# Layer 0's keys and values one chunk later, and whole steps for the empty attention steps at a layer's end

## The chip, the cores and the metric

The kernel runs on one core of one Trainium2 chip. The metric is the device time of one execution in microseconds (us); three runs were timed, and one more execution was profiled. Engines are named TensorE (PE in the profile, its weight loads PEld), VectorE (DVE), ScalarE (ACT), GpSimd (POOL) and SyncE (SP).

## The reference

Two layers of a transformer on a graph: 2708 nodes with 512 features, eight heads of 64, and a 0/1 adjacency matrix with some nine neighbours a node. Each layer is, with its own weights:

```python
q = (h @ Wq.T + bq).reshape(n, 8, 64)      # k and v likewise
scores = einsum('nhd,mhd->hnm', q, k) / sqrt(64)
scores = where(mask == 0, -1e9, scores)    # mask = adj + I
ctx = einsum('hnm,mhd->nhd', softmax(scores), v).reshape(n, 512)
h1 = layer_norm(h + ctx @ Wo.T + bo)
h2 = layer_norm(h1 + relu(h1 @ W1.T + b1) @ W2.T + b2)
```

The second layer takes h2 of the first. Everything is float32.

## The kernel before

**Tiles, blocks and chunks.** The nodes are sorted by their number of neighbours and cut into 22 tiles of 128 (the last has 20). Two tiles make a block (list `blocks`); a layer works through eleven blocks, numbered k = 0 to 10, and each block goes through the feed-forward network in 16 chunks, numbered f = 0 to 15: a chunk is 128 of the 2048 hidden units. One chunk on TensorE is four matmul calls into a PSUM tile `pf` (L1596 in the plain blocks, L1780 in the others); ScalarE evicts it with the ReLU (L1607 or L1791). The output is then summed in PSUM from the evicted chunks. In blocks 0, 1 and 10 of layer 0 that is plain (`feed_forward`, L1569). In blocks 2 to 9 it is done with seven products in place of eight for each pair of chunks (`feed_forward_by_seven`): VectorE makes sums of the evicted chunks (L1746 to L1749), and TensorE multiplies them with prepared combinations of W2, the forms (L1769), which SyncE loads from DRAM (L1731). The first products come behind chunk 5, the second behind chunk 7, and so on. In these blocks the PSUM tiles of the chunks and those of all projections and flips have two buffers each (`places_of_psum(3 - seven, ...)`), in the plain blocks three.

**What runs beside the chunks.** The loop over k and f (the body of `by_edges`) is a schedule written by hand: the engines take their instructions in the order in which the program writes them. After each chunk it writes some of these:

- The attention of later tiles, a generator (`attend`), driven by `advance(credit)`: each chunk has a credit (tables PACE, PACES, PACE7), and each step taken costs what `attend` yields, the number of gathered rows over two. A step gathers the keys and values of up to two neighbours per node (GpSimd, L1119), multiplies and sums the keys with the query on VectorE (L1156, then the scores sc, L1162), and, for the step before, takes exponentials (L1175) and weighs a part of the values on ScalarE (L1182), the rest on VectorE (L1188, L1195). When a tile is complete, VectorE sums it up (L1203 to L1218), and one step later ScalarE divides it (cx, L1226). Since each step ends the work of earlier ones, three empty steps stand behind the second tile of the order and behind the last one; an empty step costs 0.2. After the last, two small instructions set a flag (L1951).
- The output projection of the next block (`attended`, chunks 10 to 13): the attention result cx is flipped by TensorE transposes (tp, L1349), copied out of PSUM to cT by ScalarE (L1354) and multiplied with Wo (o, L626, or L621 for the 20-row tile). `until(g)` runs the attention until tile g is divided.
- In layer 0, the keys and values of the block behind (`keys_values`), a generator of four steps, taken behind chunks 5, 6, 7 and 8: flip both tiles of the normalized rows h (tp, L1349) and copy them to zT (L1354, eight pieces); project keys (k) and values (v) of the first tile (L626), evict them on VectorE (L1881) and ScalarE (L1886), and store zT and h (SyncE, L1888, L1889); the same for the second tile; scatter the rows of both tiles to DRAM (GpSimd, L1082). h comes out of VectorE's normalization (L1290) of the block that just ended.

Of the kernel before, what the change touches and what calls it, by code (L numbers as in the profile page):

```python
# [37 lines left out]
SLOTS = 2  # L38
# [449 lines left out]
def by_edges(ctx: ExitStack, tc: tile.TileContext, x, xT, adj, layers, out, redo):  # L488
# [639 lines left out]
    def asked(n, g):  # L1128

        r = size(g)  # L1130
        if g in own:
            return own.pop(g)
        if n == 0 and not all_made:
            return None
        q = at.tile([P, DM], F32, tag="q", name="q", bufs=QB)
        fetch(n, q, q_d[n], g)
        return q

    def chunks_of(g):
        S = CAPS[g]  # L1140
        k = (S + SLOTS - 1) // SLOTS
        cuts = [-(-S * i // k) for i in range(k + 1)]
        return [(g, a, b - a) for a, b in zip(cuts, cuts[1:])]
# [102 lines left out]
    def loads(n):  # L1246

        ready = []
        for g, s0, c in (chunk for g in order for chunk in chunks_of(g)):
            r = size(g)  # L1250
            kv = rows_of_keys(n)
            for s in range(s0, s0 + c):
                load = gather(kv[:r, s - s0, :], kv_d[n], idx[:r, g, s : s + 1])
                for move in written[n]:
                    tc.add_manual_dep(
                        load.ins,
                        move.ins.name,
                        mybir.DependencyInfo(
                            mybir.DependencyClass.Sync, mybir.DependencyReason.DATA
                        ),  # L1260
                        reason="every row of keys is in its place",
                    )
                written[n].clear()
            ready.append(kv)
            if len(ready) > EARLY:
                yield ready.pop(0)
        yield from ready
# [638 lines left out]
    order = [g for block in blocks for g in block]  # L1906

    def attend(n, got):

        peak = small.tile([P, NT], F32, tag="peak", name="peak", bufs=1)  # L1910
        nc.vector.memset(peak, 0.0)
        loaded = loads(n)
        steps = []
        for g in order:
            cuts = chunks_of(g)
            steps += [(g, s0, c, i, i + 1 == len(cuts)) for i, (_, s0, c) in enumerate(cuts)]
            if g == order[1]:
                steps += [None] * 3
        steps += [None] * 3
        kv = next(loaded)  # L1920
        yield 0.0
        q, later = asked(n, order[0]), None
        done = [None] * 3
        for k, step in enumerate(steps):
            if step:
                g, s0, c, i, last = step
                if i == 0:
                    while q is None:
                        q = asked(n, g)
                        if q is None:  # L1930
                            yield None
                    t, q = Tile(g, q), None
                if k > 0:
                    kv = next(loaded)
                t.weights(kv, s0, c)
                if q is None and g != order[-1]:
                    q, later = later or asked(n, order[order.index(g) + 1]), None
                if g == order[-3] and i == 2:
                    later = asked(n, order[-1])
                done.append((t, kv, s0, c, last))  # L1940
            else:
                done.append(None)
            t3, t2, t1 = done[-4:-1]
            if t1:
                t1[0].weigh(*t1[1:4])
            if t2 and t2[-1]:
                t2[0].sums(peak)
            if t3 and t3[-1]:
                got[t3[0].g] = t3[0].divided()
            yield c / SLOTS if step else 0.2  # L1950
        nc.vector.tensor_reduce(flags[:, 4 + n : 5 + n], peak, AX.X, ALU.max)  # L1951
        nc.vector.tensor_scalar(
            flags[:, 4 + n : 5 + n], flags[:, 4 + n : 5 + n], SAFE, None, ALU.is_le
        )
# [30 lines left out]

    got = {}
    ahead = attend(0, got)
    early = {}

# [38 lines left out]
    behind, pool = None, []  # L2028
    for n in range(NL):
        last = n == NL - 1  # L2030
        nxt = None if last else Layer(n + 1, layers[n + 1])
        if n > 0:
            streamed = now.queries(order[10:16])
            got = {}
            ahead = attend(n, got)
            for j in (5, 6):
                now.query(*pool.pop(0))
# [40 lines left out]
        for k, block in enumerate(blocks):  # L2078
            more = k + 1 < NB
# [13 lines left out]
            for f, zs in enumerate(working):  # L2093
# [4 lines left out]
                        added_row(h, size(g), now.e1b2)  # L2098
                if tail and f in TAILS[k > FORMED[n] + 1]:
                    next(tail)  # L2100
                if f in (5, 6, 7, 8) and behind:
                    next(behind)
                if more and n == 0 and f == 5 + 2 * (k == 0):
                    xbs = now.residuals(blocks[k + 1])
# [75 lines left out]
            if not last:  # L2180
                behind = now.keys_values(block, zs)
            if more:
                hs = hs_next
        if not last:
# [9 lines left out]
            behind = None  # L2194
# [7 lines left out]
def gnn_transformer(tc: tile.TileContext, x, xT, adj, layers, out):  # L2202

    nc = tc.nc
    with tc.tile_pool(name="result", bufs=1) as result:
        redo = result.tile([1, 1], I32, name="redo")  # L2210
        again = by_edges(tc, x, xT, adj, layers, out, redo)
        with tc.If(again > 0):
            by_rows(tc, x, xT, adj, layers, out)
# [41 lines left out]
```

## Time and profile before

| | |
|---|---|
| time, median of 3 runs | 1817.57 us (1815.81 to 1818.39) |
| profiled execution, its own time | 1817.08 us |
| its span from first to last instruction | 1815.1 us |
| mean granted clock of TensorE | 0.998 |
| ScalarE, VectorE, GpSimd busy | 55%, 81%, 47% of the span |
| moved by DMA | 426.74 MB, mean 235 GB/s |

A row of the timeline gives the start in us from the span's start, the duration, the engine, the line, the operation with output<-input, and the count of instructions merged; in brackets the idle time of the engine just before, and what ended it. A matmul's duration overlaps the next one's, so what a matmul takes of TensorE is read from start to start. A row of the list of waits gives the waiting operation, what it waited for, then the total in us, the times and the longest.

### The profile page before, as it was taken

Reading aid. Unit: us, or ns where it says so; the run is one execution under the profiler, and the core shown is the slowest. Engines: PE = TensorE matmul, PEld = TensorE weight load, DVE = VectorE, ACT = ScalarE, POOL = GpSimd, SP = SyncE. Lnnn points to the kernel's source line nnn. Section 1 sums busy time; section 2 is a strip of 40 time slices with the busy share of each in tenths; the row PEclk is TensorE's granted clock in tenths of the full one; section 3 lists DMA queues with packets and bytes.
Section 4 is the critical chain, followed back from the end, with each engine's and each line's share of the span. In section 5 each row is a group of like instructions: output and inputs, shape, how many; then the busy total and the mean of one; then the engine's idle time right before and its main releaser. Section 6 shows DMA issues by size and latency. Waiting matters only on the chain. (4 is left out here: it accounts for less than half of the span.)

```text
span 1815.1 us, 23887 instructions
## 1 busy us (share of the span) xinstructions
PE 1791.5 (99%) x6839; PEld 1214.6 (67%) x6839; DVE 1463.3 (81%) x2599; ACT 1001.1 (55%) x3397; POOL 855.4 (47%) x830
## 2 busy tenths in 40 slices
PE   9999999999999999999999999999999999999997
PEld 4444456666777867777677644666666888788786
DVE  4987778988989889799896267988888899989933
ACT  5771436645555555555653104677776677767631
POOL 3333755534454544454540132556665665655312
PEclk9999999999999999999999999999999999999999
DMA  9997987757676675666752777967867787877531
GB/s 335 369 344 252 374 284 245 230 181 241 203 238 220 203 259 192 208 220 202 241 194 73 242 285 272 319 193 256 279 186 263 243 264 237 293 225 234 173 94 36
DMA packets 186728, 426.74 MB, mean 235 GB/s; under 512 B 20550, under 2 KB 83898, under 8 KB 186584
## 3 DMA queue, kind: packets, MB, share of 16 engines
q0 software_dynamic: 76992, 264.49, 44.0%
q1 hardware_dynamic: 99434, 139.01, 22.5%
q10 hardware_dynamic: 10158, 21.61, 3.1%
q8 instruction: 56, 0.92, 0.2%
q14 instruction: 88, 0.72, 0.1%
HBM read 357.13 MB, written 57.11 MB: 228 GB/s over the span
## 5 line engine op out<-in xcount | busy, mean ns | idle before, releaser
L1119 POOL DMA_INDIRECT kv<-kv_d,listed x420 | 526.0, 1252 | 307.2 <-DVE acc L1195 145.8
L1780 PE MATMUL pf<-hT,w 128*128 128x256 f32 x1792 | 407.2, 379 | 2.1 <-ACT ft L1791 2.1
L1780 PEld LDWEIGHTS pf<-hT,w 128*128 128x128 f32 x1792 | 339.2, 190 | 59.2 <-issue 11.0
L1182 ACT ACTIVATE kv<-kv,p 128x64 f32<-128x64 f32 x1232 | 311.0, 335 | 5.0
L1156 DVE TENSOR_TENSOR kv<-kv,q 128x1024 f32<-128x1024 f32 (+1 forms) x222 | 257.1, 1158 | 14.1 <-DMA q<-q_d,ident_i 10.9
L1162 DVE TENSOR_REDUCE sc<-kv 128x16 f32<-128x1024 f32 (+1 forms) x222 | 258.0, 1162 | 7.6
L1195 DVE TENSOR_TENSOR acc<-acc,kv 128x1024 f32<-128x1024 f32 (+2 forms) x178 | 205.6, 1155 | 49.6 <-ACT kv L1182 36.9
L1596 PEld LDWEIGHTS pf<-hT,w 128*128 128x128 f32 x1024 | 178.5, 190 | 55.3 <-issue 34.6
L1596 PE MATMUL pf<-hT,w 128*128 128x256 f32 (+1 forms) x1024 | 214.6, 357 | 0.1
L1791 ACT ACTIVATE ft<-pf,b 128x256 f32<-128x256 f32 x168 | 78.1, 466 | 214.1 <-PE pf L1780 211.4
L1569 PE MATMUL a<-w,ft 128*128 128x512 f32 x416 | 194.6, 592 | 0.0
L1175 ACT ACTIVATE p<-sc,listed 128x8 f32<-128x8 f32 x420 | 103.6, 295 | 127.9 <-DVE sc L1162 116.5
L1281 POOL TENSOR_TENSOR rd<-va,mhalf 128x1 f32<-128x1 f32 (+1 forms) x48 | 43.8, 913 | 230.8 <-DVE va L1279 230.7
L626 PE MATMUL o<-wo,cT 128*128 128x512 f32 x336 | 151.0, 593 | 0.3 <-ACT cT L1354 0.3
L1188 DVE TENSOR_TENSOR kv<-kv,p 128x512 f32<-128x512 f32 (+1 forms) x178 | 123.6, 694 | 4.8 <-ACT p L1175 4.5
L1569 PEld LDWEIGHTS a<-w,ft 128*128 128x128 f32 x416 | 77.7, 190 | 57.5 <-issue 52.0
L626 PEld LDWEIGHTS o<-wo,cT 128*128 128x128 f32 x336 | 63.4, 190 | 69.3 <-issue 59.6
L1331 POOL TENSOR_SCALAR va<-sq 128x1 f32<-128x1 f32 (+1 forms) x40 | 17.2, 429 | 188.4 <-ACT xb L1324 101.9
L751 DVE MAX8 tops<-code 128x8 f32<-128x247 f32 (+2 forms) x242 | 78.8, 400 | 28.0 <-ACT code L746 27.9
L1226 ACT ACTIVATE cx<-acc,su 128x64 f32<-128x64 f32 (+1 forms) x352 | 88.2, 333 | 11.2 <-DVE su L1218 6.2
L1182 ACT ACTIVATE acc<-kv,p 128x64 f32<-128x64 f32 (+1 forms) x352 | 88.8, 335 | 1.4
L746 ACT ACTIVATE code<-aj 128x1354 bf16<-128x1354 int32 (+1 forms) x44 | 73.5, 1724 | 23.7 <-POOL aj L740 19.0
(258 smaller groups left out, 2793.8 us busy)
## 6 DMA issues: line engine op xcount, KB each, us to landing
forms<-form_d SPq DMA_DIRECT2D x294, 128.0 KB, 3.8
aj<-in_adj SPq DMA_DIRECT2D x42, 677.0 KB, 6.3
kv_d<-kvs ACTq DMA_DIRECT2D x21, 512.0 KB, 7.4
h<-ln_b POOLq DMA_DIRECT2D x41, 256.0 KB, 7.0
xg<-in_xT SPq DMA_DIRECT2D x19, 512.0 KB, 8.0
w<-in_W SPq DMA_DIRECT2D x16, 512.0 KB, 6.4
kv<-kv_d,listed POOLq DMA_INDIRECT x420, 6.5
zT_d<-zT SPq DMA_DIRECT2D x22, 256.0 KB, 5.3
```

The source lines that it names most:

```text
L626: nc.tensor.matmul(o[:r], xs(c), wm[:, c, :], start=(c == 0), stop=(c == NC - 1))
L1119: return nc.gpsimd.indirect_dma_start(out=to, out_offset=None, in_=table[:, :], in_offset=bass.IndirectOffsetOnAxis(ap=s, axis=0), bounds_ ...
L1156: nc.vector.tensor_tensor(kv[:r, :c, :DM], kv[:r, :c, :DM], self.q[:r].unsqueeze(1).to_broadcast([r, c, DM]), ALU.mult,)
L1162: nc.vector.tensor_reduce(self.sc[:r, s0 : s0 + c, :], kv[:r, :c, :DM].rearrange("p s (h d) -> p s h d", d=DK), AX.X, ALU.add,)
L1175: nc.scalar.activation(p[:r, s, :], self.sc[:r, s, :], AF.Exp, bias=minus[:r, g, s : s + 1])
L1182: nc.scalar.activation(to[:, i, hd], kv[:r, i, DM + h * DK : DM + (h + 1) * DK], AF.Copy, scale=p[:r, s0 + i, h : h + 1],)
L1188: nc.vector.tensor_tensor(to[:, 0, :].rearrange("p (h d) -> p h d", d=DK), kv[:r, 0, DM:].rearrange("p (h d) -> p h d", d=DK), p[:r, s0, : ...
L1195: nc.vector.tensor_tensor(self.acc[:r, :c, :], self.acc[:r, :c, :], kv[:r, :c, DM:], ALU.add)
L1226: nc.scalar.activation(cx[:r, hd], self.acc[:r, 0, hd], AF.Copy, scale=self.su[:r, h : h + 1])
L1569: nc.tensor.matmul(a[:r, cols], fts[f][:, c0 : c0 + r], self.w2[f // 2][:, f % 2, cols], start=(f == 0), stop=(f == NFC - 1),)
L1596: nc.tensor.matmul(pf[:, :w], self.w1[f // 2][:, c, f % 2 * P : f % 2 * P + P], hT[:, c, :w], start=(c == 0), stop=(c == NC - 1),)
L1780: nc.tensor.matmul(pf[:, :W], self.w1[j][:, c, f % 2 * P : f % 2 * P + P], hT[:, c, :], start=(c == 0), stop=(c == NC - 1),)
```

## The change

Two lines of the schedule:

```diff
@@ attend
-            yield c / SLOTS if step else 0.2
+            yield c / SLOTS if step else 0.2 if g == order[1] else 1.0
@@ the loop over blocks and chunks
-                if f in (5, 6, 7, 8) and behind:
+                if behind and more <= f - 5 < 4 + more:
                     next(behind)
```

`more` is true in all blocks but the last. So in blocks 1 to 9 of layer 0 the four steps of the keys and values come behind chunks 6, 7, 8 and 9; in block 10 they stay at 5 to 8, and layer 1 has none. The empty steps at the end of a layer (three, in both layers) cost 1.0 each, so that they are spread over more chunks; those behind the second tile keep 0.2.

What stands where now, at three places. TensorE in block 8 of layer 0, from chunks 4 and 5 (w_1589 is theirs) over the first products (L1769) and chunks 6 and 7 (w_1671) to the first keys; before:

```order
L1780 MATMUL pf<-hT,w_1589 128x256 x8
L1349 MATMUL tp<-ident,h 128x128 x8
L1769 MATMUL a_7033<-forms,ft 128x256
L1769 MATMUL c_6896<-forms 128x256
L1769 MATMUL c_6897<-forms,ft 128x256
L1769 MATMUL c_6896<-w_1465,ft 128x256
L1769 MATMUL a_7032<-w_1465,ft 128x256
L1769 MATMUL c_6897<-w_1465,forms 128x256
L1769 MATMUL a_7032<-w_1465,forms 128x256
L1780 MATMUL pf<-hT,w_1671 128x256 x4
L626 MATMUL k<-wk,zT 128x512 x4
L626 MATMUL v<-wv,zT 128x512 x4
```

The flips stood ahead of the first products, and one chunk ahead of the keys. And after the change:

```order
L1780 MATMUL pf<-hT,w_1589 128x256 x8
L1769 MATMUL a_7012<-forms,ft 128x256
L1769 MATMUL c_6896<-forms 128x256
L1769 MATMUL c_6897<-forms,ft 128x256
L1769 MATMUL c_6896<-w_1465,ft 128x256
L1769 MATMUL a_7011<-w_1465,ft 128x256
L1769 MATMUL c_6897<-w_1465,forms 128x256
L1769 MATMUL a_7011<-w_1465,forms 128x256
L1780 MATMUL pf<-hT,w_1671 128x256 x4
L1349 MATMUL tp<-ident,h 128x128 x8
L1780 MATMUL pf<-hT,w_1671 128x256 x4
L626 MATMUL k<-wk,zT 128x512 x4
```

The flips now stand behind the products and chunk 6, and only chunk 7 lies between them and the keys. ScalarE at the same place, as a difference; the forms row is the eviction of chunk 5, the ft row that of chunk 6, kvs the copy of the first tile's values:

```order
 L1791 ACTIVATE forms<-pf,b_1158 128x256
+L1175 ACTIVATE p<-sc,listed 128x8 x2
+L1182 ACTIVATE kv<-kv,p 128x64 x8
+L1226 ACTIVATE cx<-acc,su 128x64 x8
+L1791 ACTIVATE ft<-pf,b_1158 128x256
 L1354 ACTIVATE zT<-tp,bo 128x128 x8
-L1175 ACTIVATE p<-sc,listed 128x8 x2
-L1182 ACTIVATE kv<-kv,p 128x64 x8
-L1226 ACTIVATE cx<-acc,su 128x64 x8
-L1791 ACTIVATE ft<-pf,b_1158 128x256
-L1886 COPY kvs<-v 128x512
```

The copies to zT moved behind an attention step, a division and an eviction. The third place is ScalarE in block 9 of layer 0, chunks 9 to 11, before (the two forms rows are the evictions of chunks 10 and 11):

```order
L1791 ACTIVATE ft<-pf,b_1158 128x256
L1226 ACTIVATE cx<-acc,su 128x64 x8
L1791 ACTIVATE forms<-pf,b_1158 128x256
L1354 ACTIVATE cT<-tp,bv 128x20 x4
L1791 ACTIVATE forms<-pf,b_1158 128x256
L1354 ACTIVATE cT<-tp,bv 128x128 x4
```

and after:

```order
L1791 ACTIVATE ft<-pf,b_1158 128x256
L1791 ACTIVATE forms<-pf,b_1158 128x256
L1354 ACTIVATE cT<-tp,bv 128x20 x4
L1791 ACTIVATE forms<-pf,b_1158 128x256
L1226 ACTIVATE cx<-acc,su 128x64 x8
L1354 ACTIVATE cT<-tp,bv 128x128 x4
```

The division of the layer's last tile moved from ahead of chunk 10's eviction to behind chunk 11's, and so behind the 20-row tile's cT.

## Prediction

> **What bounds the kernel now.** I read the page first, then the list of who waited for whom on TensorE, then the timeline of TensorE, ScalarE and VectorE in layer 0, block by block. From the page, the busy line and the costliest group of GpSimd; from the list of waits, the three rows on layer 0:
>
> ```profile
> PE 1791.5 (99%) x6839; PEld 1214.6 (67%) x6839; DVE 1463.3 (81%) x2599; ACT 1001.1 (55%) x3397; POOL 855.4 (47%) x830
> L1119 POOL DMA_INDIRECT kv<-kv_d,listed x420 | 526.0, 1252 | 307.2 <-DVE acc L1195 145.8
> ```
> ```profile
> PE tp L1349 <- DVE h L1290: 3.1, 4, 1.0
> PE o L621 <- ACT cT L1354: 2.4, 1, 2.4
> PE pf L1780 <- ACT ft L1791: 2.1, 4, 0.8
> ```
>
> A busy TensorE need not be at its peak, but its timeline in layer 0 shows matmuls issued end to end for hundreds of microseconds, broken only by a few waits near 1 us and one of 2.4. So TensorE is a wall: work that only changes places on it is free, and the time moves by the waits that go and the waits that come. ScalarE is at 55%, but it takes its instructions in the order written, and TensorE depends on it. This is block 5 of layer 0 on TensorE (start, duration, line, output, count), from the end of chunk 5:
>
> ```profile
> 632.81 1.04 PE L1349 MATMUL tp<-ident,h 128*128 128x128 f32 x8
> ...
> 636.71 1.89 PE L1780 MATMUL pf<-hT,w 128*128 128x256 f32 x8
> 638.43 3.60 PE L626 MATMUL k<-wk,zT 128*128 128x512 f32 x8
> 641.87 3.60 PE L626 MATMUL v<-wv,zT 128*128 128x512 f32 x8
> 645.30 1.89 PE L1780 MATMUL pf<-hT,w 128*128 128x256 f32 x8
> ```
>
> Between starts: the flips of both tiles with the first products take 3.90 us, chunk 6 takes 1.72, keys and values of one tile 6.87. Nothing waits here. Now the same place on ScalarE:
>
> ```profile
> 636.01 0.45 ACT L1791 ACTIVATE forms<-pf,b 128x256 f32<-128x256 f32 x1
> 636.36 2.12 ACT L1354 ACTIVATE zT<-tp,bo 128x128 f32<-128x128 f32 x8
> 638.36 0.50 ACT L1175 ACTIVATE p<-sc,listed 128x8 f32<-128x8 f32 x2
> ...
> 640.83 0.45 ACT L1791 ACTIVATE ft<-pf,b 128x256 f32<-128x256 f32 x1
> ```
>
> ScalarE evicts chunk 5, copies the flipped tiles out of PSUM (zT, eight pieces) and only then does the exponentials and weighting of an attention step, 2.47 us from their start to the eviction of chunk 6. The keys need zT, and have it in time although ScalarE runs some 3 us behind TensorE.
>
> **The change, part by part.** *The keys and values, blocks 1 to 9 of layer 0.* No matmul is added. On TensorE the flips move from behind chunk 5 to behind chunk 6, and the keys from behind chunk 6 to behind chunk 7. On ScalarE the copies to zT move behind the attention step of chunk 5 and behind the eviction of chunk 6. Two effects follow.
>
> First, what goes. In blocks 2 and 3 the second flip waits for the normalized rows h:
>
> ```profile
> 403.91 0.60 PE L1349 MATMUL tp<-ident,h 128*128 128x128 f32 x4
> 405.36 0.66 PE L1349 MATMUL tp<-ident,h 128*128 128x128 f32 x4 [0.85 <-DVE h L1290]
> ...
> 480.49 0.60 PE L1349 MATMUL tp<-ident,h 128*128 128x128 f32 x4
> 482.06 0.66 PE L1349 MATMUL tp<-ident,h 128*128 128x128 f32 x4 [0.98 <-DVE h L1290]
> ```
>
> A chunk later h is there: 0.85 + 0.98 = 1.83 us go at this place. (The first products then stand where the flips stood; they need sums that VectorE makes right after h, so part of this wait is only handed on. That lies ahead of the keys and is inside the wait worked out next.)
>
> Second, what comes. Call E the moment when chunk 5 is issued, which in this trace is the start of the tp row. Ahead of the keys TensorE now has flips and products (3.90), chunk 6 (1.72) and chunk 7 (1.73): it arrives at E + 7.35. When is zT there? The attention step of chunk 5 needs the scores that VectorE makes in the step before. Block 8 shows that wait, with the division of a finished tile (cx) behind it; it has cx ahead of the eviction, as block 7 has:
>
> ```profile
> 864.97 1.22 DVE L1162 TENSOR_REDUCE sc<-kv 128x16 f32<-128x1024 f32 x1
> ```
> ```profile
> 866.23 0.49 ACT L1175 ACTIVATE p<-sc,listed 128x8 f32<-128x8 f32 x2 [1.04 <-DVE sc L1162]
> ...
> 868.68 2.00 ACT L1226 ACTIVATE cx<-acc,su 128x64 f32<-128x64 f32 x8
> 870.59 0.45 ACT L1791 ACTIVATE ft<-pf,b 128x256 f32<-128x256 f32 x1
> ```
>
> From the start of the score row to the exponential 1.26 us; to the eviction of chunk 6 2.47 (with the division 870.59 - 866.23 = 4.36); to zT 0.35; then the pieces. How many must be there? The last tile of layer 0 shows a keys matmul that waited for zT, on ScalarE and on TensorE:
>
> ```profile
> 1062.47 1.14 ACT L1354 ACTIVATE zT<-tp,bo 128x128 f32<-128x128 f32 x4 [1.71 <-PE tp L1349]
> ```
> ```profile
> 1063.66 3.70 PE L626 MATMUL k<-wk,zT 128*128 128x512 f32 x8 [0.25 <-ACT zT L1354]
> ```
>
> It began 0.05 us after the fourth piece. In blocks 2 to 9 the code gives a second reason: the projections have two PSUM buffers, and the keys take the buffer out of which the first flipped tile is copied. So half of the 2.12 us counts: 1.06, and 0.05. Together 1.26 + 2.47 + 0.35 + 1.06 + 0.05 = 5.19 us from the score row, 7.08 with a division. The wait is (score - E) + 5.19 - 7.35. The rows of E and of the score for the other blocks (blocks 2, 3, 5 and 8 have one or both above):
>
> ```profile
> 557.36 1.04 PE L1349 MATMUL tp<-ident,h 128*128 128x128 f32 x8
> 709.31 1.04 PE L1349 MATMUL tp<-ident,h 128*128 128x128 f32 x8
> 785.81 1.04 PE L1349 MATMUL tp<-ident,h 128*128 128x128 f32 x8
> 861.41 1.04 PE L1349 MATMUL tp<-ident,h 128*128 128x128 f32 x8
> 936.86 1.04 PE L1349 MATMUL tp<-ident,h 128*128 128x128 f32 x8
> ```
> ```profile
> 408.58 1.22 DVE L1162 TENSOR_REDUCE sc<-kv 128x16 f32<-128x1024 f32 x1
> 485.29 1.22 DVE L1162 TENSOR_REDUCE sc<-kv 128x16 f32<-128x1024 f32 x1
> 559.63 1.22 DVE L1162 TENSOR_REDUCE sc<-kv 128x16 f32<-128x1024 f32 x1
> 636.25 1.22 DVE L1162 TENSOR_REDUCE sc<-kv 128x16 f32<-128x1024 f32 x1
> 712.74 1.22 DVE L1162 TENSOR_REDUCE sc<-kv 128x16 f32<-128x1024 f32 x1
> 788.76 1.22 DVE L1162 TENSOR_REDUCE sc<-kv 128x16 f32<-128x1024 f32 x1
> 939.45 1.22 DVE L1162 TENSOR_REDUCE sc<-kv 128x16 f32<-128x1024 f32 x1
> ```
>
> Score behind E: 4.67, 4.80, 2.27, 3.44, 3.43, 2.95, 3.56, 2.59 us in blocks 2 to 9. Less 2.16 (less 0.27 in blocks 7 and 8, with the division): waits of 2.51, 2.64, 0.11, 1.28, 1.27, 2.68, 3.29 and 0.43, in all 14.2 us. These sums are an estimate from rows of one execution. Block 1 has three PSUM buffers and, with the plain second product, more matmuls between flip and keys: no wait there, by my reading.
>
> Do the waits come back later? From the end of the second tile's values on, ScalarE must copy them first, so its next evictions hang on TensorE's own time; the attention steps stand in the same chunks as before. I find the same distance between the engines at the next block's start, and so no return. The waits of 0.8 us for an eviction (the pf row of the list) come from two attention steps and a division in chunk 8; these stay behind the copy of the values on ScalarE, so I leave the waits as they are.
>
> *The other queues.* GpSimd's two scatters of a block move with the step, behind one or more gathers that stood behind them, and still wait for the last copy of the values. GpSimd sat idle for 307 us ahead of its gathers (the L1119 row), and they are issued chunks ahead: cost 0; if that cover were gone, a late gather would hold VectorE, and through it the scores, by at most what the scatter comes later, once a block: 1.73 us for chunk 7 and about 3 for the second products. SyncE's stores of zT and h move behind three loads of forms; nobody waits for them within a block: 0. VectorE's additions of the key bias move one place; it has to wait there for the second keys, ahead of work that it could have done, but it is in step again by the copy of the values: 0.
>
> *The empty steps.* In layer 0, block 9, the last tile's division moves behind the eviction of chunk 11, and the 20-row tile's cT no longer stands behind it:
>
> ```profile
> 971.42 2.02 ACT L1226 ACTIVATE cx<-acc,su 128x64 f32<-128x64 f32 x8 [2.54 <-DVE flags L1951]
> 973.70 0.75 ACT L1354 ACTIVATE cT<-tp,bv 128x20 f32<-128x20 f32 x4
> ```
> ```profile
> 974.01 1.52 PE L621 MATMUL o<-wo,cT 128*20 128x512 f32 x8 [2.41 <-ACT cT L1354]
> ```
>
> That wait of 2.41 goes. But right behind that projection (1.5 us) TensorE flips the divided tile itself, whose sums now stand behind one more group of VectorE's, about 1.2 us. I take a new wait of 1.2 there: gain 1.2, with bounds 0 and 2.41. In layer 1 the division moves behind two evictions that come ahead of any need, and two tiny flag instructions move: 0, and the list of waits names none of them.
>
> The sum: 14.2 - 1.8 - 1.2 = 11.2 us slower. Against the profiled execution, 1817.08, that is 1828.3; its time stands 0.5 below the median of the runs, 1817.57, so against the median 1828.8. Two tenths of a per cent, 3.6 us, is about what a measurement of this kernel can tell from no change.
>
> **The rivals.**
>
> *The keys start on the first piece.* In the row of the 20-row tile above, the projection began 0.31 us after its first cT piece, not after the fourth. If the keys did so, three pieces (0.8 us) fall off each wait, all of the two small ones: 5.3 us less, +5.9, 1823.5. Against it stand the row at 1063.66 and the shared PSUM buffer. Chance 0.16.
>
> *Faster: the scores come earlier.* Should the later keys leave VectorE and ScalarE ahead at the end of each block, the scores of the next one land sooner against E. The point that decides is 2.16 us behind E (0.27 with a division): from there the keys never wait, 1.8 and 1.2 go, and perhaps the evictions' 1.6 of 2.1: 3 to 4.6 us faster, about 1814. For it: VectorE's 81% leaves room. Against it: not one of eight rows is under 2.16 now, and two would have to gain 2.5. Chance 0.08.
>
> *Nothing.* If VectorE's chain were what paces the blocks, TensorE's new waits would be slack and the time stay within 2 us, 1817 to 1819. Against it: TensorE's wall without gaps. Chance 0.09.
>
> *The clock.* A waiting TensorE might lose its granted clock. This stretch, behind the longest wait of layer 0 (columns: window, length, busy PE, PEld, DVE, ACT, POOL, granted clock, DMA share, GB/s), shows none lost:
>
> ```profile
> 974.00:985.00 11.00, 10.99 (x46) 7.43 (x47) 7.45 (x15) 2.42 (x9) 0.94 (x1) 1.00 0.17 49
> ```
>
> If the waits of 2.7 and 3.3 us in blocks 7 and 8 halved it for the keys and values behind them, 6.87 us would double twice: 13.7 us more, 1842. Chance 0.03. The Trainium skill, "TensorE: Matmul & The Clock Gate", section "What's actually happening", states this rule: about 3.4 us of idleness gate the array to half rate. By that rule waits under 3.4 us stay at full rate, the trace agrees with its clock of 1.00 behind 2.41, and no run here shows a longer one in the midst of the work.
>
> **How the numbers follow.** My forecast has 0.64: 1828.8, by itself from 1824 to 1833, if each of the six larger waits is off by half a microsecond or so and the empty steps go either way. The range of 1820 to 1834 takes in the first-piece rival; it leaves out the cases of nothing, of faster and of the clock, 0.20 together. Slower: 0.64 + 0.16 + 0.03 = 0.83. Same 0.09, faster 0.08.
>
> **What would show it.** In the list of TensorE's waits: a new row of keys (k, L626) waiting for ScalarE's zT, six to eight times, 10 to 14 us in all with what the first products wait for VectorE, longest about 2.7 in blocks 7 and 8; the tp row down by two cases; the o L621 row gone, a tp row for cx in its place. Blocks 7 and 8 should each be about 3 us longer, block 4 not at all. I am wrong if the keys start without a wait, if such waits are there but the blocks are no longer, or if layer 1 changes by more than 1 us.

## The result and the profile after

The changed kernel takes 1827.93 us (median of 6 runs, 1827.17 to 1831.53), the kernel before 1817.49 beside it (6 runs): ratio 1.0056, 95% interval 1.0045 to 1.0067, slower by 10.2 us by that ratio (10.4 between the medians). The profiled execution took 1827.17 us with a span of 1825.3, against 1817.08 and 1815.1 before: 10.1 us more.

TensorE's busy time hardly moved, and its share fell by one point. From the page of the changed kernel:

```profile
PE 1793.9 (98%) x6839; PEld 1212.8 (66%) x6839; DVE 1464.5 (80%) x2599; ACT 1002.2 (55%) x3397; POOL 859.9 (47%) x830
```

The list of what TensorE waited for, changed kernel (us in all, times, longest):

```profile
PE k L626 <- ACT zT L1354: 7.6, 8, 2.4
PE c L1769 <- DVE forms L1748: 2.9, 4, 1.7
PE pf L1780 <- ACT ft L1791: 2.4, 4, 0.9
PE c L1769 <- issue: 1.6, 1, 1.6
...
PE tp L1349 <- DVE h L1290: 1.2, 2, 0.6
```

Seven of the eight waits of keys for zT are new (the eighth, 0.25 us at the layer's last tile, was there before), and so are the five of the first products for VectorE's sums, 11.8 us together. The 1.64 us that the list puts down to issue belong to the five: they stand at the first products of block 2 and end 0.11 us behind VectorE's sum L1748. The tp row is down from four cases to two, and the 2.41 us of o L621 are gone. The mechanism shows in full in block 8; TensorE, from the first products:

```profile
869.79 0.59 PE L1769 MATMUL a<-forms,ft 128*128 128x256 f32 x2
...
876.15 1.89 PE L1780 MATMUL pf<-hT,w 128*128 128x256 f32 x8
880.49 3.70 PE L626 MATMUL k<-wk,zT 128*128 128x512 f32 x8 [2.45 <-ACT zT L1354]
```

And the two engines that feed it, VectorE's score and ScalarE:

```profile
873.36 1.22 DVE L1162 TENSOR_REDUCE sc<-kv 128x16 f32<-128x1024 f32 x1
```
```profile
874.61 0.49 ACT L1175 ACTIVATE p<-sc,listed 128x8 f32<-128x8 f32 x2 [3.08 <-DVE sc L1162]
875.13 2.02 ACT L1182 ACTIVATE kv<-kv,p 128x64 f32<-128x64 f32 x8
877.06 2.01 ACT L1226 ACTIVATE cx<-acc,su 128x64 f32<-128x64 f32 x8
878.97 0.46 ACT L1791 ACTIVATE ft<-pf,b 128x256 f32<-128x256 f32 x1
879.32 2.14 ACT L1354 ACTIVATE zT<-tp,bo 128x128 f32<-128x128 f32 x8
```

The score lies 3.57 us behind the first products (E), ScalarE begins 1.25 behind the score, evicts chunk 6 another 4.36 later, starts the copy 0.35 after that, and the keys start at 880.49, 0.1 after half of the copy. TensorE was done with chunk 7 at 877.88 (876.15 and the 1.73 us of a chunk, from start to start).

The block lengths follow. The flips to hT close blocks 6, 7 and 8; before:

```profile
765.09 1.04 PE L1349 MATMUL tp<-ident,h 128*128 128x128 f32 x8
...
840.69 1.04 PE L1349 MATMUL tp<-ident,h 128*128 128x128 f32 x8
...
916.14 1.04 PE L1349 MATMUL tp<-ident,h 128*128 128x128 f32 x8
```

and after:

```profile
770.72 1.04 PE L1349 MATMUL tp<-ident,h 128*128 128x128 f32 x8
...
849.07 1.04 PE L1349 MATMUL tp<-ident,h 128*128 128x128 f32 x8
...
927.98 1.04 PE L1349 MATMUL tp<-ident,h 128*128 128x128 f32 x8
```

Block 7 grew from 75.60 to 78.35 us (+2.75), block 8 from 75.45 to 78.91 (+3.46). By the same kind of row blocks 2 to 6 grew by 1.60, 1.43, 0.32, 1.53 and 1.54.

### The profile page after: what moved, and what is told of

The parts are those of the page before. It is cut to its first block, busy times and chain, and to the rows that moved or that the text cites. A ratio compares the mean times of both kernels' runs of the same rounds, so it can differ in the third digit from the quotient of the medians.

```text
span 1825.3 us, 23899 instructions
## 1 busy us (share of the span) xinstructions
PE 1793.9 (98%) x6839; PEld 1212.8 (66%) x6839; DVE 1464.5 (80%) x2599; ACT 1002.2 (55%) x3397; POOL 859.9 (47%) x830
## 4 chain that ended last, share of the span: by engine, by line
PE 52%; DVE 7%; ACT 4%; issue 3%; POOL 1%; DMA 1%; POOLq 0%; DVEq 0%; ACTq 0%
PE pf L1780 11%; PE pf L1596 7%; PE a L1569 6%; PE c L1769 6%; PE o L626 6%; PE a L1769 4%; PE q L626 3%; PE k L626 3%; PE v L626 2%; ACT kv L1182 2%; PE tp L1349 1%; DVE kv L1156 1%; DVE sc L1162 1%; PE a L1800 1%; PE a L1804 1%
```

## The experiments

The theory from the prediction: what counts is how late zT is copied in ScalarE's queue against the moment at which TensorE wants the keys. Rivals came up on the way: that keys and values one chunk later cost something by themselves, that one chunk between flip and keys is too short whatever ScalarE does, and that the granted clock has a part in it. Each kernel is compared with the kernel before on the same chip.

**Keys alone.** The changed kernel without the edit of the empty steps:

```diff
-            yield c / SLOTS if step else 0.2 if g == order[1] else 1.0
+            yield c / SLOTS if step else 0.2
```

> Keys and values a chunk later, the empty steps as in the kernel before. Theory: this half alone is the loss, 13.9 us of waits ahead of the keys less the 1.8 of the flips' waits for h, 12.1 us, some 1829.6, ratio 1.0067; the 2.41 wait of the 20-row tile's projection for cT is back in the list. Rival: the empty steps gave nothing, so this kernel stands with the changed one, 1827.5 to 1828.5.

Measured: 1831.65 us, ratio 1.0076 (1.0062 to 1.0090). The 1.0067 lies inside, but the profiled execution had something that my sum had left out and only a rival had named. TensorE at the keys of block 7 and block 8:

```profile
801.47 5.19 PE L626 MATMUL k<-wk,zT 128*128 128x512 f32 x8 [2.44 <-ACT zT L1354]
...
881.92 5.40 PE L626 MATMUL k<-wk,zT 128*128 128x512 f32 x8 [2.45 <-ACT zT L1354]
```

The waits are those of the changed kernel to 0.01 us, yet the eight matmuls take 5.19 and 5.40 us instead of 3.70. From start to start the two rows take 5.02 and 5.24 us where the changed kernel's took 3.54, so 1.48 and 1.70 us are lost. The windows behind the first wait show why (length, then busy times, then the granted clock, DMA share, GB/s):

```profile
796.00:797.00 1.00, 1.00 (x9) 0.90 (x9) 1.00 (x4) 0.97 (x5) 0.54 (x2) 1.00 0.98 357
801.50:804.50 3.00, 3.00 (x4) 1.45 (x5) 2.83 (x7) 2.97 (x13) 2.17 (x2) 0.50 0.87 305
```

The granted clock was 1.00 ahead of the wait and 0.50 behind it. In the changed kernel's own trace it stayed at full:

```profile
801.60:804.00 2.40, 2.40 (x6) 1.17 (x7) 2.26 (x6) 2.37 (x11) 1.62 (x2) 1.00 0.87 335
```

So a wait of 2.44 us loses the clock in one execution and not in another; more on this below. Without the two losses, 3.2 us, the ratio would be near 1.0058, with the rival; so this run does not decide whether the empty steps gave anything. The next one does.

**The empty steps alone.**

```diff
-                if behind and more <= f - 5 < 4 + more:
+                if f in (5, 6, 7, 8) and behind:
```

> The empty steps by whole steps, keys and values as in the kernel before. Theory: a gain of 1.2 us (the 2.41 wait goes, about 1.2 comes back at the flips of the divided tile), some 1816.3, ratio 0.9993; no keys wait for zT. Rival: the divided tile is awaited just as long as the 20-row tile was, and the time stays at 1817.5, ratio 1.0000.

Measured: 1816.26, ratio 0.9988 (0.9979 to 0.9997), a gain of 2.2 us with an interval of 0.5 to 3.8. The place itself, this kernel:

```profile
969.53 1.99 PE L1780 MATMUL pf<-hT,w 128*128 128x256 f32 x8
971.46 1.05 PE L621 MATMUL o<-wo,cT 128*20 128x512 f32 x8
972.99 0.80 PE L1349 MATMUL tp<-ident,cx 128*128 128x128 f32 x2 [0.48 <-ACT cx L1226]
...
974.59 0.60 PE L1769 MATMUL a<-forms,ft 128*128 128x256 f32 x2
```

From chunk 10's matmuls to the first products 5.06 us; before, the same stretch ran from 969.61 to 975.96, 6.35 us. So 1.3 us are won here, against a forecast of 1.2: the projection no longer waits, and the flips of the divided tile trickle in as its pieces are divided.

**The flips stay, the keys come later.** Flips behind chunk 5 as before, the rest one chunk later as in the change:

```diff
-                if behind and more <= f - 5 < 4 + more:
+                if behind and f in ((5, 7, 8, 9) if more else (5, 6, 7, 8)):
```

> As the changed kernel, but the flips stay behind chunk 5 while keys, values and scatters still come one chunk later: two chunks now lie between flip and keys, and ScalarE copies zT ahead of chunk 5's attention step again. Theory (the copy's place in ScalarE's queue is the cost, not the later keys): the row of keys waiting for zT is gone, the two waits of the flips for h (1.8) are back, and the time is that of the empty steps alone, some 1816.3, ratio 0.9993. Rival (keys and values a chunk later cost by themselves, through the copies of the values that now stand later on ScalarE and the evictions behind them): the time stays near 1828.

Measured: 1819.12, ratio 1.0002 (0.9993 to 1.0011). The theory holds for the larger part: of the loss against the empty steps alone (1.0056 or more against 0.9988) about four fifths go with the copy's old place. But 1816.3 was not reached. The list of TensorE's waits:

```profile
PE k L626 <- ACT kvs L1886: 3.6, 3, 1.8
PE tp L1349 <- DVE h L1290: 3.1, 4, 1.0
...
PE k L626 <- ACT zT L1354: 0.2, 1, 0.2
```

The second tile's keys now wait for ScalarE's copy of the first tile's values, in blocks 3, 7 and 8 (0.97, 1.81 and 0.79 us). So the rival is right to that amount: the values a chunk later cost about 2.5 us by themselves (1.0002 against 0.9988). What the copy waited for, the profile doesn't name; in block 7 it stood 3.43 us with ScalarE idle and began 0.07 us after the end of an addition of VectorE's attention work:

```profile
805.23 1.23 DVE L1195 TENSOR_TENSOR acc<-acc,kv 128x1024 f32<-128x1024 f32 x1
```
```profile
806.53 0.58 ACT L1886 COPY kvs<-v 128x512 f32<-128x512 f32 x1 [3.43 <-issue]
```

The kernel gives a reason: kvs, the tile that the copy writes, is one of five buffers under one tag (`KVB = 5`), which the attention's gathered rows kv share, and the addition that ended just before reads such a row. VectorE's eviction of the keys (L1881), which writes the same tile, began behind that addition too, at 806.91. So the copy probably waited for a buffer that VectorE's attention still held; no run here changes the number of buffers to show it.

The changed kernel doesn't show this wait; by my reading because its first keys start late, and the rest with them.

**An attention step a chunk earlier.** The changed kernel with chunk 4's and chunk 5's credit one chunk earlier, so that nothing of the attention stands between the evictions of chunks 5 and 6:

```diff
-    (0.0,) * 4 + (0.6,) + (1.3,) * 4 + (0.6,) * 2 + (0.0,) * 2 + (0.5, 0.8, 2.4),
+    (0.0,) * 3 + (0.6, 1.3, 0.0) + (1.3,) * 3 + (0.6,) * 2 + (0.0,) * 2 + (0.5, 0.8, 2.4),
```

> As the changed kernel, but the attention steps of chunks 4 and 5 are asked for in chunks 3 and 4 in blocks 2 to 9, so that no attention step stands between the evictions of chunks 5 and 6 on ScalarE. Theory: the waits of the keys for zT (7.6 us, 8 times) go, and with the flips a chunk later those for h as well: 1814.5 to 1818, the top of it if the score that VectorE now makes a chunk earlier holds up h and the first products in blocks 2 and 3. Rival (the one chunk between flip and keys is too short whatever stands on ScalarE): the keys still wait 5 us or more, and the time is above 1823.

Measured: 1827.55, ratio 1.0048 (1.0034 to 1.0061). Both expectations missed, the theory by its time and the rival by its wait. The list:

```profile
PE pf L1780 <- ACT forms L1791: 3.3, 2, 2.1
PE pf L1780 <- issue: 3.3, 6, 2.1
...
PE k L626 <- ACT zT L1354: 0.2, 1, 0.2
```

The keys don't wait any more, but the chunks do, a place earlier. ScalarE in block 7:

```profile
794.86 0.49 ACT L1175 ACTIVATE p<-sc,listed 128x8 f32<-128x8 f32 x2 [3.13 <-DVE sc L1162]
...
797.31 2.00 ACT L1226 ACTIVATE cx<-acc,su 128x64 f32<-128x64 f32 x8
799.22 0.45 ACT L1791 ACTIVATE forms<-pf,b 128x256 f32<-128x256 f32 x1
```

And TensorE and VectorE there:

```profile
791.72 0.59 PE L1769 MATMUL a<-forms,ft 128*128 128x256 f32 x2
...
799.73 0.48 PE L1780 MATMUL pf<-hT,w 128*128 128x256 f32 x1 [2.10 <-ACT forms L1791]
```
```profile
793.60 1.22 DVE L1162 TENSOR_REDUCE sc<-kv 128x16 f32<-128x1024 f32 x1
```

VectorE makes the score behind the normalization and the first sums. Asked for a chunk earlier, it came 1.88 us behind the first products; in the changed kernel it was 2.95. That is 1.07 us won, where the step was moved by a chunk of 1.73. Step and division now hold up the eviction of chunk 5, and chunk 7 waits 2.10 us for its buffer. So the order on ScalarE decides who waits. Where the lateness comes from is so far only a reading: the step has only chunks beside it, where keys and values (6.87 us) stood before.

**One chunk more between flips and keys.**

```diff
-                if behind and more <= f - 5 < 4 + more:
+                if behind and f in ((6, 8, 9, 10) if more else (5, 6, 7, 8)):
```

> As the changed kernel, with keys, values and scatters one chunk later still: two chunks between flips and keys, as in the run where the flips stayed, but with the flips behind chunk 6. Theory of the prediction (only the distance between zT's copy in ScalarE's queue and the keys counts): the eight waits of the keys, 8.6 us in the changed kernel, fall by 1.73 us each, to 1.8 in all; the waits of the first products stay; some 1821. Second theory, formed on the run with the step a chunk earlier (an attention step needs a long piece of TensorE's work beside it, and keys and values were that piece; without it TensorE catches up with ScalarE wherever the step stands): the waits come back as waits of pf for an eviction or of keys for the copied values, and the time stays at 1826 or above.

Measured: 1835.88, ratio 1.0095 (1.0080 to 1.0109), some 14 us above what the distance alone would give. TensorE's list:

```profile
PE k L626 <- ACT kvs L1886: 12.0, 5, 5.1
...
PE k L626 <- DVE kvs L1881: 2.5, 3, 1.0
...
PE k L626 <- ACT zT L1354: 0.2, 1, 0.2
```

The wait for zT is gone, as the distance says, but the second tile's keys wait in all eight blocks, up to 5.06 us, for the first tile's values or keys to be taken out of PSUM. The second theory told the level right.

**The attention steps a chunk later too.**

```diff
-    (0.0,) * 4 + (0.6,) + (1.3,) * 4 + (0.6,) * 2 + (0.0,) * 2 + (0.5, 0.8, 2.4),
+    (0.0,) * 5 + (0.6,) + (1.3,) * 4 + (0.6,) * 2 + (0.0, 0.5, 0.8, 2.4),
```

> As the changed kernel, with the attention steps of chunks 4 to 10 one chunk later in blocks 2 to 9 of layer 0, so that they stand to keys and values as they did before. Second theory (a step needs keys and values beside it): the waits of the keys for zT go (7.6 us to under 2), those of the first products for VectorE shrink with the load that leaves VectorE ahead of them, and what is left is a possible wait of the output projections at the end of the block, which now have a chunk less: 1815 to 1820. Rival (one chunk between flip and keys is too short by itself): the keys still wait 5 us or more, above 1824.

Measured: 1836.41 (1830.88 to 1839.05), ratio 1.0088 (1.0073 to 1.0104). The waits for zT went as expected, the time did not:

```profile
PE c L1769 <- DVE forms L1748: 9.1, 6, 3.5
PE o L626 <- ACT cT L1354: 6.0, 4, 2.2
...
PE k L626 <- ACT zT L1354: 0.3, 1, 0.3
```

The output projections behind chunk 10 now wait for divided tiles (a possible price that I had named without a number), and VectorE, later at the end of each block, comes later to the first products' sums of the next, where I had expected relief (at the end of block 2 it begins to add up the block's output 3.1 us later than in the changed kernel, while TensorE is 1.2 us later there). The steps can't follow the keys: the end of the block holds them.

**All but blocks 7 and 8, and blocks 7 and 8 alone.** The change left out in these two blocks, and then made only there (with the empty steps spaced in both):

```diff
-                if behind and more <= f - 5 < 4 + more:
+                if behind and (more and k not in (7, 8)) <= f - 5 < 4 + (more and k not in (7, 8)):
```
```diff
-                if behind and more <= f - 5 < 4 + more:
+                if behind and (k in (7, 8)) <= f - 5 < 4 + (k in (7, 8)):
```

> The change without blocks 7 and 8, where the keys waited 2.44 and 2.45 us. Theory: the time falls by those blocks' waits, 2.60 + 3.25 us, to some 1822.1, ratio 1.0025; no wait of over 2 us is left in blocks 1 to 8, the granted clock stays at 1.00 behind each, and the executions of this kernel scatter less than those of the changed one (1827.2 to 1831.5). Rival (those waits are given back later in the block, or the loss comes from elsewhere): 1825 or above.

> The change of keys and values in blocks 7 and 8 alone, with the empty steps by whole steps. Theory: the empty steps alone (0.9988) plus the two blocks' waits, 5.9 us, and 0 to 3.4 us of half clock behind them: 1822 to 1825, ratio 1.0020 to 1.0039. With the run without these two blocks it has to add up to the changed kernel. Rival (the blocks are not independent): outside of that.

Measured: without the two blocks 1821.81, ratio 1.0018 (1.0009 to 1.0026); with them alone 1822.73, ratio 1.0025 (1.0015 to 1.0036). Both are as expected, and they add up: 0.18 + 0.25, and 0.12 for the gain of the empty steps that both contain, is 0.55% against 0.56 for the change. Each of these figures has an interval of about 0.1 either way; within that the blocks are independent, and their waits are not given back. The trace of the second has one wait with loss of clock and one without:

```profile
797.01 3.70 PE L626 MATMUL k<-wk,zT 128*128 128x512 f32 x8 [2.44 <-ACT zT L1354]
...
875.97 5.40 PE L626 MATMUL k<-wk,zT 128*128 128x512 f32 x8 [2.44 <-ACT zT L1354]
```

**The second tile flipped first.**

```diff
-            turn(0)
             if block != blocks[-1]:
                 turn(1)
+            turn(0)
+            zTs.reverse()
```

> As the changed kernel, but the second tile of a block is flipped ahead of the first, so that the first keys need all eight pieces of the copy to zT instead of four. Theory: each of the eight waits of blocks 2 to 9 grows by four pieces, 1.06 us, 8.5 us in all: 1836.4; the waits of blocks 7 and 8 come to 3.5 us, and if a wait of that length always takes the granted clock to half for the keys behind it, 1.6 to 1.8 us more for each of the two, near 1840. Rival (the keys wait for the PSUM buffer alone, which comes free with the tile flipped first): 1828.

Measured: 1832.19, ratio 1.0072 (1.0059 to 1.0085). Neither: the waits grew, but by 0.26, not by 1.06. The keys of blocks 2, 7 and 8:

```profile
412.96 3.70 PE L626 MATMUL k<-wk,zT 128*128 128x512 f32 x8 [0.78 <-ACT zT L1354]
...
802.71 5.40 PE L626 MATMUL k<-wk,zT 128*128 128x512 f32 x8 [2.69 <-ACT zT L1354]
...
883.62 3.70 PE L626 MATMUL k<-wk,zT 128*128 128x512 f32 x8 [2.70 <-ACT zT L1354]
```

In the changed kernel these were 0.52, 2.44 and 2.45. A piece of the copy takes 2.12 / 8 = 0.265 us. So the keys wait until the tile that was flipped first has left its PSUM buffer (four pieces), and then for the first piece of their own zT, which is the fifth here.

**The changed kernel again.** No edit.

> The changed kernel once more, for its scatter and a second trace. First theory (a wait of 2.44 us in blocks 7 and 8 takes the granted clock to half for the keys behind it in some executions and not in others, as the traces of the kernel without the empty steps and of the one with the second tile first show, at 1.6 to 1.8 us a time): executions spread over some 1826 to 1832, and if this trace has a loss, it stands in the keys row behind one of those two waits. Rival (those losses belong to those kernels): the granted clock is 1.00 behind both waits again, and the executions lie within 2 us of each other.

Measured: 1829.56 (1826.10 to 1833.13), ratio 1.0070 (1.0058 to 1.0082). The trace shows the waits of 2.44 and 2.45 us with a clock of 1.00 behind both, as the rival has it; the scatter of 7.0 us is as the theory has it, and the three quickest executions had a mean granted clock of 0.998, the three slowest 0.996 or 0.997. In the kernel without blocks 7 and 8 ten of eleven executions lie within 2.0 us, all at 0.998. That this kernel's own executions lose clock there is likely, but no trace of it shows one. The last section shows what decides whether a wait loses it.

**Better than both.** The empty steps alone, with chunk 8's credit lowered from 1.3 to 0.9 and chunk 9's raised from 0.6 to 1.0, aimed at the two waits of pf in blocks 5 and 6 that the prediction had left as they are:

```diff
-    (0.0,) * 4 + (0.6,) + (1.3,) * 4 + (0.6,) * 2 + (0.0,) * 2 + (0.5, 0.8, 2.4),
+    (0.0,) * 4 + (0.6,) + (1.3,) * 3 + (0.9, 1.0, 0.6) + (0.0,) * 2 + (0.5, 0.8, 2.4),
```

> The empty steps alone, with 0.4 of chunk 8's credit moved to chunk 9, so that blocks 5 and 6 no longer take two attention steps and a division behind chunk 8 (block 9 moves one step as well). Theory: the two waits of pf for an eviction (0.78 and 0.79 there, 0.95 from start to start each) go, 1.9 us, some 1814.4, ratio 0.9977 to 0.9980. Rival (what goes there comes back at the output projections behind chunk 10, which wait for the divided tiles): no gain over the empty steps alone, 1816.3, ratio 0.9988.

Measured: 1814.56, ratio 0.9983 (0.9974 to 0.9991). The row of pf waiting for ft, 2.0 us in three cases with the empty steps alone, has left the list, and the output projections have only this row, as small as before (0.3):

```profile
PE o L626 <- ACT cT L1354: 0.4, 1, 0.4
```

It beats the kernel before by 3.1 us (1.6 to 4.7), somewhat less than forecast (0.9977 to 0.9980). That it beats the empty steps alone is not shown: the list says that a wait went, but the two intervals overlap.

## Why the prediction came out

The forecast was 1828.8, the measurement 1827.93, and the waits that it named are the ones that came.

*The waits ahead of the keys.* Forecast for blocks 2 to 9: 2.51, 2.64, 0.11, 1.28, 1.27, 2.68, 3.29, 0.43, in all 14.2 us. Measured from start to start, first products and keys together: 2.49, 2.58, 0.1, 1.20, 1.20, 2.60, 3.25, 0.47, in all 13.9. The chain from score to zT and the split by the division held to a tenth of a microsecond, and the kernels with and without blocks 7 and 8 show that these waits carry the time.

*Half of the copy.* The number (1.06 and 0.05) was right, and one of the two reasons for it wrong. With the second tile first, the keys need one piece of their own zT, not four; it is the shared PSUM buffer that makes them wait for half the copy. The first-piece rival was right about the data and wrong about the time, for the same reason.

*What goes.* The h waits at tp in blocks 2 and 3 are gone (1.83). The empty steps gave 1.3 us alone and in the changed kernel 1.5 at their place (4.86 us from chunk 10 to the first products, before 6.35), forecast 1.2. The pf waits that I left as they are grew by 0.1 each. What is left of the blocks' growth, some 1.2 us, is a term that the sum had left out: the matmuls right behind a wait start more slowly. From start to start, eight matmuls of keys take 3.54 us behind these waits and 3.44 without one, and a pair of the first products 0.50 to 0.54 instead of 0.43, some 1.3 us over the eight blocks. That, and a wait too short for the list, is also why block 4, forecast not to grow at all, grew by 0.32. From the flips near 308 us in both traces to the keys of the layer's last tile the trace is 11.7 us longer, against a forecast of 11.2.

*Nothing elsewhere.* Layer 1 became 0.7 us shorter, inside the bound of 1 us (two waits of its queries, 1.61 and 0.55, became one of 1.23); another 0.8 lies ahead of the flips near 308 us, where nothing was changed. 11.7 - 0.7 - 0.8 gives the 10.2 by which the span grew.

*The clock.* This rival was priced wrongly. I held that waits of 2.7 us would keep the clock, by the row behind the 2.41. They keep it in some executions: of the ten waits of 2.44 to 2.70 us ahead of the keys of blocks 7 and 8 in five traces, four were followed by half clock. The prediction's reading that waits under 3.4 us stay at full rate does not hold in these runs, where 2.44 us were enough. The price was wrong too: 1.5 to 1.7 us each, not 6.87, since full clock came back after 3.4 us. So the forecast's agreement within 1 us owes something to which executions made up the median: the second set of the same kernel has 1829.56.

*What the theory lacked.* It priced one hand-over, zT to the keys. The runs with the flips kept and with a wider gap show a second one behind it, the first tile's values out of PSUM for the second tile's keys; that the changed kernel hides it because the first wait has already made TensorE late fits its list, where no such wait stands, but no run separates the two.

## What to carry to other kernels

When TensorE is a wall, a long piece of its work is the cover under which slower engines catch up; before moving it, work out for each engine in program order when it delivers what the moved piece needs, and do so for every hand-over behind it, PSUM buffers included. Moving the other engine's work instead renames the wait: in three arrangements here the wait for zT went to nothing and came back as one for an eviction, a value copy or a sum. A wait of 2.4 us on TensorE can cost more than its length, and not in every execution, so compare several before you believe a difference of 2 us.

## What the hardware did that was not expected

The granted clock fell to 0.50 behind waits well under 3 us. Beside the ten waits above: in the run with the attention steps later, two waits of 2.23 us for cT stood ahead of output projections; behind the first the clock fell and the eight matmuls took 5.40 us, behind the second it did not:

```profile
678.98 5.40 PE L626 MATMUL o<-wo,cT 128*128 128x512 f32 x8 [2.23 <-ACT cT L1354]
```

There waits of 3.55 us and of 2.43 us lost clock as well, and in the run with the wider gap one of 5.06, but one of 3.04 didn't, nor did those of 2.17, 2.22, 2.35 and 2.41 us.

The traces show what separates them: where a wait lies. Read in steps of 0.2 us, each stretch at half clock lasts 3.4 us (behind the 5.06 us twice as long), and all the falls of one trace lie on a grid of 3.413 us: with the keys alone they come at 801.09 and 883.01 us and, at the kernel's end, at 1821.67 us, that is 24 and 275 steps apart. Laid back over a trace from the fall at its end, the grid cuts the time into windows. Between 200 and 1785 us, in all thirteen traces, the clock fell right behind the eight windows in which TensorE was busy for 1.41 us or less, and behind no window in which it was busy for 1.52 us or more. The run with blocks 7 and 8 alone has a window of either kind, around its two waits of 2.44 us (the first number behind the comma is TensorE's busy time); behind the first the clock stayed at 1.00, at the end of the second it fell:

```profile
795.45:798.86 3.41, 1.85 (x5) 0.90 (x6) 3.17 (x7) 3.38 (x14) 1.00 (x2) 1.00 0.90 320
873.96:877.37 3.41, 1.40 (x4) 0.68 (x5) 3.17 (x7) 3.38 (x15) 0.99 (x2) 1.00 0.53 163
```

So the wait of 3.04 us kept full clock because it was split between two windows (1.97 and 1.82 us busy), and the first of the two waits of 2.23 us lost it because it lay in one (1.18 us busy). The grid lies differently against the kernel in each trace, so the same wait is cut differently each time.

The Trainium skill, "TensorE: Matmul & The Clock Gate", section "What's actually happening", describes a window of about 3.4 us that runs freely and doesn't start with the kernel's work. The free run of the window and the length of a loss (3.4 us at half rate) agree with these runs; that it takes a whole idle window does not, since windows with up to 1.41 us of work were followed by half clock. The measurement decides: by these traces the limit lies between 1.41 and 1.52 us of work in a window.
